# A graph layer in fp32: the add of an edge part between the two products of an older unit on VectorE

## The chip, the cores and the metric

The kernel runs on one core of a Trainium2 chip. Five engines work side by side, each through its own instructions in order: TensorE (PE, matrix products into PSUM), VectorE (DVE), ScalarE (ACT), GpSimd (POOL, here the issuer of gathers) and SyncE (SP, here the issuer of plain DMAs). They wait for each other by semaphores. The metric is the device time of one execution in microseconds, as the median of several runs. The profile is of one execution and has a span, from the first to the last instruction, and a time of its own.

## What is computed

One layer of a graph network over 6250 nodes and 206250 edges with 256 features, all in fp32:

```python
h = relu(layernorm(x))
polarity = clip(edge_attr[:, 0:1], 0.0, 1.0)
e = relu(edge_attr[:, 1:] @ W_e1.T + b_e1) @ W_e2.T + b_e2
edge_emb = (e * (polarity + 0.01)) @ W_le.T + b_le
msg = relu(h[src] + edge_emb)
aggr = segment_sum(msg, dst, num_segments=6250)
out = x + (relu(layernorm((h + aggr) @ W_g1.T + b_g1) * ln_g + ln_b) @ W_g2.T + b_g2)
```

(the layer normalisation's gain and offset stand in the last line for short). The edges are sorted by `dst`. The kernel multiplies `W_e2` and `W_le` together once, so that an edge needs two matrix products: the first layer, 64 to 256, and the edge part, 256 to 256. The edge's factor, `polarity + 0.01`, is applied afterwards, as a product with a scalar for each partition.

## The kernel before

**Tiles.** Edges come in tiles of 128. Two tiles make a unit, 806 in all, two units a block, two blocks a pair. Six blocks make a group, whose messages are summed into one PSUM tile.

**PSUM.** Seven banks (`banks`, `BANKS = 7`) form a ring. Each new use takes the next bank; the matmul that writes it waits for the reader of seven uses ago. An eighth bank, `pd`, holds the sums of two groups.

**A unit's way.**
- `first_layer(q)` (L292): the first layer of a pair, on TensorE. It takes four banks, two for each half `c`. The four results are evicted with bias and Relu, three on ScalarE (L308) and one on VectorE (L305). The first matmul of each half waits for the readers of both its banks.
- `edge_part(u)` (L325): four matmuls into one bank. Then the *add* (L331) on VectorE: bank plus bias, written to `msg[u]` in SBUF, and with it the bank is free.
- `gather` (L634): two indirect DMAs on GpSimd fetch the rows `h[src]` (with `b_le` in them) into `hg[u]`. They are issued in step with TensorE (`in_step`, called at the end of `edge_part`).
- `whole(u)`: two *products* (L685) on VectorE, each `hg = msg * factor + hg` on 128x256, then one Relu (L690) on ScalarE over both.
- `add_up` (L703): selection matrices times `hg`, the sums of a block, on TensorE. `add_pairs` decides how many pairs are summed, from `made`, the number of units whose products are issued.

**The order.** It is written out by hand; the scheduler is off. The main loop goes over u, and each step issues for all engines: `forward(u)` (the edge part of unit u and, in some units, a turn), a *piece*, the products of one or more older units, a part of the node work, and later moves. The products run behind the edge part by `lag` units, which falls from 18 to 1 over the run:

```python
lag = max(LEAST, LEAD - RAW - u // SHRINK) + (by_two(u // 4) and (u + 1) % 8 == TURN)
ready_for = min(u + 1 - lag, 5 * (u + 1 - LEAD) // 4)
while made < ready_for:
    gathers(made + 1)
    whole(made)
    made += 1
```

**Turns.** Between the sixth pair and the sixth from the end (`by_two`), two pairs are turned at once, in units with `u % 8 == 1`: the first layer of one pair (four banks), the sums, the first layer of the next pair (four banks), and two loads of 256 KB on SP's queue (`load_pair`). In the unit before, `u % 8 == 0`, `lag` is one more and no products are issued; in the turn's unit two units' products are. "Unit 0" to "unit 7" below mean `u % 8`.

**Pieces.** `piece()` takes one waiting small step of VectorE: a selection matrix for a block (L663, from `rest`, filled when sums are issued) or a step of the node work that is due (L800, L230). It is called once in a unit, and once more when over six are waiting.

**Node work.** Windows of 128 nodes go through a transpose (L166), a product (L181), normalisation on VectorE and ScalarE (L189 to L193), a transpose (L199), and a last product (L212, L217). `due()` issues one such part in a unit, but none in units 0 and 1. Each takes a bank of the ring.

Of the kernel before, what the change touches and what calls it, by code (L numbers as in the profile page):

```python
# [11 lines left out]
AF = mybir.ActivationFunctionType  # L12
ALU = mybir.AluOpType
# [23 lines left out]
NP = -(-NB // 2)  # L37
# [3 lines left out]
LEAD = 22  # L41
LEAST = 1
# [4 lines left out]
SHRINK = 44  # L47
RAW = 4
# [3 lines left out]
TURN = 1  # L52
# [48 lines left out]
def gnn_kernel(ctx: ExitStack, tc: tile.TileContext, x, src_c, dst_c, dst_r, pol_c, raw_t, w_e1t, w_e2,  # L101
               w_let, w_g1t, w_g2t, vec_c, row_v, x_t, out):
    nc = tc.nc
# [23 lines left out]
    pol_s = const.tile([P, NT], F32, name="pol_s")  # L127
# [106 lines left out]
    NU = 2 * NB  # L234
    fast = ExitStack()
    fast.enter_context(tc.manual_schedule())
    with fast:
# [9 lines left out]
        raw, sel, e1, hg, msg, ms = {}, {}, {}, {}, {}, {}  # L247
# [65 lines left out]
        def plain(u):  # L313

            return u < LEAD and u % 3 == 1

        def edge_part(u):

            nonlocal last_z
            b, v = divmod(u, 2)  # L320
            pz = ps()
            for i in range(2):
                k = (2 * v + i) * P
                for c in range(2):
                    last_z = nc.tensor.matmul(pz[:, i, :], e1[b][:, c, k:k + P], wc_s[:, c, :], start=c == 0, stop=c == 1)  # L325
            ps.wrote(last_z)
            msg[u] = msg_p.tile([P, 2, D], F32, name="msg")
            if plain(u):
                ps.read(nc.scalar.activation(msg[u], pz, AF.Copy))
            else:  # L330
                ps.read(nc.vector.tensor_add(msg[u], pz, bc_s))  # L331
            if v == 1:
                e1.pop(b)
            paced(EDGE, last_z)

        last_z = None
        sums = lambda last: None
        paced = lambda us, behind: None

        def by_two(q):  # L340
            return FEW <= q < NP - FEW
# [65 lines left out]
        with tc.tile_pool(name="p1", bufs=4) as p1, tc.tile_pool(name="p1x", bufs=11) as p1x:  # L407
# [76 lines left out]
            for k in range(len(parts) + 1):  # L484
                last = len(parts) - 1
# [128 lines left out]
        with tc.tile_pool(name="hg", bufs=HG - RAW) as hg_p, tc.tile_pool(name="ms", bufs=4) as ms_p, \  # L614
# [7 lines left out]
            done = {}  # L622
# [18 lines left out]
            def gathers(last):  # L641

                while got < 2 * min(NU, last):
                    gather()
# [29 lines left out]
                elif rest:  # L674
                    rest.popleft()[1]()

            def whole(u):

                m = msg.pop(u)
                if u < RAW:  # L680
                    nc.vector.tensor_add(hg[u], hg[u], ble_b.rearrange("p (o d) -> p o d", o=1).to_broadcast([P, 2, D]))
                if plain(u):
                    nc.vector.tensor_add(m, m, bc_s)
                for i in range(2):
                    product = nc.vector.scalar_tensor_tensor(hg[u][:, i, :], m[:, i, :], pol_s[:, 2 * u + i:2 * u + i + 1],  # L685
                                                   hg[u][:, i, :], op0=ALU.mult, op1=ALU.add)
                    if u == NU - 1:
                        nc.scalar.activation(hg[u][:, i, :], hg[u][:, i, :], AF.Relu)
                if u < NU - 1:
                    done[u] = product, nc.scalar.activation(hg[u], hg[u], AF.Relu)  # L690

            def add_up(b, newest=()):

# [41 lines left out]
            def add_pairs(last=False):  # L735

                nonlocal summed
                whole_groups = []
                pairs = 0
                while summed + pairs < NP and min(4 * (summed + pairs) + 4, NU) < made + last:  # L740
                    pairs += 1
                for _ in range(pairs):
                    newest = done.get(4 * summed + 3, ())
                    for b in (2 * summed, 2 * summed + 1):
                        if b < NB:
                            whole_groups.append(add_up(b, newest))
                            newest = ()
                            if b % L == 0 and group_of(b) + 2 < NG:
                                rest.extend(select(group_of(b) + 2))
                    summed += 1  # L750

                for g in whole_groups:
                    keep(g)
# [158 lines left out]
                    todo.setdefault(now + 1, deque()).extendleft(reversed(fns))  # L912

            gathers(RAW + 1)
            sums = add_pairs
            paced = in_step
            def strips():
                rows_of_edges()
# [13 lines left out]
            for u in range(LEAD, NU):  # L932
                now = u
                forward(u)

                if u >= NU - 24:
                    gathers(4 * summed + HG)

                piece()
                lag = max(LEAST, LEAD - RAW - u // SHRINK) + (by_two(u // 4) and (u + 1) % 8 == TURN)  # L940
                ready_for = min(u + 1 - lag, 5 * (u + 1 - LEAD) // 4)
                while made < ready_for:
                    gathers(made + 1)
                    whole(made)
                    made += 1
                due()
                for fn in moves.pop(now, []):
                    fn()
                if len(rest) > 6:
                    piece()  # L950
                if u == NU - 24:
                    for w in range(NW):
                        if groups_of(w)[-1] == NG - 1:
                            late[w] = node_work(w, True)
                if u == LEAD + 60:
                    flag = nc.values_load(bad_i[0:1, 0:1], min_val=0, max_val=4 * P)
# [209 lines left out]
```

## Time and profile before

| | |
|---|---|
| median of three runs | 2563.11 us (2563.05 to 2566.45) |
| the profiled execution, own time | 2555.42 us |
| its span | 2553.7 us |
| its mean granted TensorE clock | 0.964 |
| ScalarE, Relu of the products (L690) | 805 of 631 ns, 507.6 us |
| VectorE, selection matrices (L663) | 403 of 344 ns, 138.6 us |
| TensorE, edge parts (L325) | 1506.0 us in 6448 instructions |
| TensorE, first layer (L292) | 462.0 us in 1612 instructions |
| TensorE, sums (L703) | 266.0 us in 3216 instructions |

A row of groups names the line, the engine, the operation, what is written and read, the count; after the bar the busy time in us and the mean of one in ns; after the second bar the engine's idle time just before such instructions and what ended it. A row of the timeline has start in us, length, engine, line, operation, count, and in brackets the idle time before it with its releaser. Rows that begin with an engine and a line only are from a view of one line's waiters: total us and times. A row of windows has the stretch, then busy us (and count) of PE, PEld, DVE, ACT and POOL, the granted clock, the DMA share and GB/s. fp32 matmuls stand in the trace as two instructions each. "remote" and "issue" are waits whose end the profile could not place.

### The profile page before, as it was taken

To read this page: it belongs to the slowest core of one execution; us is meant where nothing else is said; L and a number is where in the kernel's file an instruction comes from. 1 tells how busy PE (TensorE), PEld (TensorE's weight loads), DVE (VectorE), ACT (ScalarE), POOL (GpSimd) and SP (SyncE) were. 2 spreads that over 40 slices of the span, in tenths; PEclk is the share of its full clock that TensorE was granted. 3 is DMA by queue.
4 is the path that set the end of the run, shared out by engine and by line. 5 is a ranking of instruction groups with operands and counts; after the bars stand their busy time and mean duration, and the time that the engine had idled before them with its cause. 6 is when DMAs were issued, how large, how long until landed. Compare 5 with 4: busy or idle time off the path is not lost.

```text
span 2553.7 us, 36839 instructions
## 1 busy us (share of the span) xinstructions
PE 2312.4 (91%) x11940; PEld 1603.9 (63%) x11940; DVE 1599.9 (63%) x3705; ACT 1012.7 (40%) x1804; POOL 1630.2 (64%) x1675
## 2 busy tenths in 40 slices
PE   9899889998999989899899989999989999898968
PEld 6666666665656666666666666666656666565646
DVE  7776556665656656565656665666656666666636
ACT  7443334343433434343433433433344334334323
POOL 7666666666666666666666666666666666666661
PEclk9899999999989999999999999999999999999979
DMA  9444444444444444444444444444444444443441
GB/s 306 139 123 127 116 132 131 125 126 134 129 122 137 121 122 130 133 127 116 126 129 123 132 135 118 130 124 136 135 121 124 127 129 142 120 130 114 123 119 42
DMA packets 176431, 330.30 MB, mean 129 GB/s; under 512 B 39056, under 2 KB 98281, under 8 KB 176233
## 3 DMA queue, kind: packets, MB, share of 16 engines
q0 software_dynamic: 77376, 211.39, 29.6%
q1 hardware_dynamic: 97556, 113.22, 13.7%
q10 hardware_dynamic: 1300, 3.28, 0.4%
q8 instruction: 95, 1.56, 0.3%
q14 instruction: 104, 0.84, 0.1%
HBM read 293.92 MB, written 33.82 MB: 128 GB/s over the span
## 4 chain that ended last, share of the span: by engine, by line
PE 77%; DVE 8%; issue 8%; another core or an unknown queue 3%; ACT 2%; DMA 0%; DVEq 0%; ACTq 0%
PE pz L325 48%; PE pz L292 15%; PE pd L703 8%; DVE hg L685 4%; DVE msg L331 2%; PE pz L181 2%; PE pz L212 2%; ACT hg L690 1%; PE pz L166 1%; ACT e L308 1%; DVE sel L663 1%; PE pz L199 0%; DVE xt L230 0%; DVE stb L800 0%
## 5 line engine op out<-in xcount | busy, mean ns | idle before, releaser
L634 POOL DMA_INDIRECT hg<-hb_d,src_s x1604 | 1585.3, 988 | 862.9 <-issue 519.1
L325 PE MATMUL pz<-wc_s,e 128*128 128x256 f32 x6448 | 1506.0, 387 | 60.0 <-issue 46.6
L325 PEld LDWEIGHTS pz<-wc_s,e 128*128 128x128 f32 x6448 | 1225.5, 193 | 344.1 <-issue 130.9
L690 ACT ACTIVATE hg<-hg 128x512 f32<-128x512 f32 x805 | 507.6, 631 | 980.7 <-DVE hg L685 766.0
L331 DVE TENSOR_TENSOR msg<-pz,bc_s 128x512 f32<-128x512 f32 x799 | 545.4, 685 | 379.0 <-PE pz L325 143.0
L685 DVE SCALAR_TENSOR_TENSOR hg<-msg,pol_s,hg 128x256 f32<-128x256 f32 x1612 | 696.5, 479 | 0.8 <-DMA hg<-hb_d,src_s 0.5
L292 PE MATMUL pz<-raw,we_s 64*128 64x512 f32 x1612 | 462.0, 657 | 66.6 <-DVE msg L331 30.1
L308 ACT ACTIVATE e<-pz,vecs 128x512 f32<-128x512 f32 x605 | 372.7, 684 | 256.6 <-remote 110.1
L305 DVE TENSOR_SCALAR e<-pz,vecs 128x512 f32<-128x512 f32 x201 | 150.2, 747 | 503.5 <-remote 176.4
L703 PE MATMUL pd<-hg,sel 128*32 128x256 f32 x3216 | 266.0, 398 | 71.6 <-issue 69.6
L292 PEld LDWEIGHTS pz<-raw,we_s 64*128 64x128 f32 x1612 | 152.3, 196 | 277.5 <-issue 143.5
L703 PEld LDWEIGHTS pd<-hg,sel 128*32 128x32 f32 x3216 | 118.5, 112 | 244.6 <-issue 201.2
L663 DVE SCALAR_TENSOR_TENSOR sel<-iota_w,zero_c,rel 128x128 f32<-128x128 f32 x403 | 138.6, 344 | 0.0
L718 ACT ACTIVATE ms<-pd 128x256 f32<-128x256 f32 x66 | 25.3, 384 | 246.4 <-remote 90.5
L181 PE MATMUL pz<-wg_s,hT 128*128 128x256 f32 (+1 forms) x196 | 54.0, 398 | 17.5 <-issue 7.6
L212 PE MATMUL pz<-wg_s,nT 128*128 128x256 f32 (+1 forms) x196 | 51.5, 385 | 6.4 <-ACT nT L203 4.9
L181 PEld LDWEIGHTS pz<-wg_s,hT 128*128 128x128 f32 (+1 forms) x196 | 35.1, 191 | 33.0 <-ACT hT L170 11.3
L212 PEld LDWEIGHTS pz<-wg_s,nT 128*128 128x128 f32 (+1 forms) x196 | 36.8, 190 | 13.4 <-ACT nT L203 6.4
L444 POOL TENSOR_TENSOR hb<-xt,rows_b 128x256 f32<-128x256 f32 (+1 forms) x49 | 34.1, 728 | 10.8 <-issue 4.4
L800 DVE TENSOR_TENSOR stb<-stb,ab 128x256 f32<-128x256 f32 x94 | 39.2, 417 | 2.6 <-DMA ab<-sum_d 2.6
L203 ACT ACTIVATE nT<-pz,vecs 128x128 f32<-128x128 f32 (+1 forms) x98 | 38.7, 444 | 2.4 <-PE pz L199 2.4
L230 DVE SCALAR_TENSOR_TENSOR xt<-xt,zero_c,rows_b 128x128 f32<-128x128 f32 (+1 forms) x98 | 33.6, 344 | 0.0
(108 smaller groups left out, 378.5 us busy)
## 6 DMA issues: line engine op xcount, KB each, us to landing
raw<-in_raw_t_dram SPq DMA_DIRECT2D x202, 256.0 KB
hg<-hb_d,src_s POOLq DMA_INDIRECT x1604
sum_d<-zrow SPq DMA_DIRECT2D x94, 128.0 KB
ab<-sum_d SPq DMA_DIRECT2D x94, 128.0 KB
sum_d<-ms SPq DMA_DIRECT2D x264, 32.0 KB
hb_d<-hb SPq DMA_DIRECT2D x12, 512.0 KB
xt<-in_x_dram SPq DMA_DIRECT2D x48, 128.0 KB
out_dram<-ot SPq DMA_DIRECT2D x48, 128.0 KB
```

Source lines behind the costliest of these rows:

```text
L181: z = nc.tensor.matmul(ph[:n, 0, :], aT[:, c, :n], wg1_s[:, c, :], start=c == 0 and not bias_by_pe, stop=c == 1)
L212: z = nc.tensor.matmul(po[:n, 0, :], nT[:, c, :n], wg2_s[:, c, :], start=c == 0, stop=c == 1)
L292: z[c] = nc.tensor.matmul(pe[s, c], we1_s[s * F:(s + 1) * F, c * P:(c + 1) * P], raw[q][s * F:(s + 1) * F, :], start=True, stop=True)
L305: a = nc.vector.tensor_scalar(e1[b][:, c, :], pe[s, c], be1_s[:, c:c + 1], 0.0, op0=ALU.add, op1=ALU.max)
L308: a = nc.scalar.activation(e1[b][:, c, :], pe[s, c], AF.Relu, bias=be1_s[:, c:c + 1])
L325: last_z = nc.tensor.matmul(pz[:, i, :], e1[b][:, c, k:k + P], wc_s[:, c, :], start=c == 0, stop=c == 1)
L331: ps.read(nc.vector.tensor_add(msg[u], pz, bc_s))
L634: g = nc.gpsimd.indirect_dma_start(out=hg[u][:, i, :], out_offset=None, in_=hb_d, in_offset=bass.IndirectOffsetOnAxis(ap=src_s[:, 2 * u + ...
L663: nc.vector.scalar_tensor_tensor(sel[g][:, k * S:(k + 1) * S, :], iota_w.rearrange("p (o w) -> p o w", o=1).to_broadcast([P, S, W]), zero_ ...
L685: product = nc.vector.scalar_tensor_tensor(hg[u][:, i, :], m[:, i, :], pol_s[:, 2 * u + i:2 * u + i + 1], hg[u][:, i, :], op0=ALU.mult, op ...
L690: done[u] = product, nc.scalar.activation(hg[u], hg[u], AF.Relu)
L703: z = nc.tensor.matmul(acc[g][j * W:(j + 1) * W, :], sel[g][:, k * S + j, :], m[:, j % 2, :], start=k == 0, stop=b == blocks_of(g)[-1])
```

## The change

In units 2 to 7 of the two-pair part of the run, if one unit's products are due, the first of them is issued before the add of the edge part and the second after it, inside `edge_part`. The piece, that stood between add and products, comes after both. In the turn's unit (`u % 8 == TURN`) and outside the two-pair part the products stay where they were, after `forward(u)` and the piece, but a call of `piece()` now stands between the two products of each unit. `due_at` is the old expression for what is due. `add_pairs` counts as before: inside a unit whose products were issued early, `made` is taken one lower. No operation, tile, DMA or buffer count is changed.

```diff
             msg[u] = msg_p.tile([P, 2, D], F32, name="msg")
+            half_of_products(u, 0)
             if plain(u):
                 ps.read(nc.scalar.activation(msg[u], pz, AF.Copy))
             else:
                 ps.read(nc.vector.tensor_add(msg[u], pz, bc_s))
+            half_of_products(u, 1)
...
-            def whole(u):
-
-                m = msg.pop(u)
+            def products(u, i):
+
+                if i == 0:
+                    opened(u)
+                product = nc.vector.scalar_tensor_tensor(hg[u][:, i, :], msg[u][:, i, :], pol_s[:, 2 * u + i:2 * u + i + 1],
+                                               hg[u][:, i, :], op0=ALU.mult, op1=ALU.add)
+                if u == NU - 1:
+                    nc.scalar.activation(hg[u][:, i, :], hg[u][:, i, :], AF.Relu)
+                elif i == 1:
+                    done[u] = product, nc.scalar.activation(hg[u], hg[u], AF.Relu)
+                if i == 1:
+                    msg.pop(u)
...
+            def whole(u, between=lambda: None):
+
+                products(u, 0)
+                between()
+                products(u, 1)
...
-                while summed + pairs < NP and min(4 * (summed + pairs) + 4, NU) < made + last:
+                while summed + pairs < NP and min(4 * (summed + pairs) + 4, NU) < made - eager + last:
...
+            def due_at(u):
+
+                lag = max(LEAST, LEAD - RAW - u // SHRINK) + (by_two(u // 4) and (u + 1) % 8 == TURN)
+                return min(u + 1 - lag, 5 * (u + 1 - LEAD) // 4)
+
+            def half_now(u, i):
+
+                nonlocal made, eager
+                if i == 0:
+                    eager = by_two(u // 4) and u % 8 != TURN and made < due_at(u)
+                    if eager:
+                        gathers(made + 1)
+                if eager:
+                    products(made, i)
+                    made += i
...
                 piece()
-                lag = max(LEAST, LEAD - RAW - u // SHRINK) + (by_two(u // 4) and (u + 1) % 8 == TURN)
-                ready_for = min(u + 1 - lag, 5 * (u + 1 - LEAD) // 4)
-                while made < ready_for:
+                while made < due_at(u):
                     gathers(made + 1)
-                    whole(made)
+                    whole(made, piece)
                     made += 1
```

`opened(u)` holds what `whole` did first for the earliest units (the bias of `hg` for u < 4, the bias of `msg` where ScalarE had copied it).

12 lines of the change are left out of this document (5 added, 7 removed).

## The prediction

> **What bounds the kernel now.** I read the page first: the engines' busy time, the chain that ended last, the costliest groups.
>
> ```profile
> span 2553.7 us, 36839 instructions
> PE 2312.4 (91%) x11940; PEld 1603.9 (63%) x11940; DVE 1599.9 (63%) x3705; ACT 1012.7 (40%) x1804; POOL 1630.2 (64%) x1675
> PE 77%; DVE 8%; issue 8%; another core or an unknown queue 3%; ACT 2%; DMA 0%; DVEq 0%; ACTq 0%
> L331 DVE TENSOR_TENSOR msg<-pz,bc_s 128x512 f32<-128x512 f32 x799 | 545.4, 685 | 379.0 <-PE pz L325 143.0
> L685 DVE SCALAR_TENSOR_TENSOR hg<-msg,pol_s,hg 128x256 f32<-128x256 f32 x1612 | 696.5, 479 | 0.8 <-DMA hg<-hb_d,src_s 0.5
> L305 DVE TENSOR_SCALAR e<-pz,vecs 128x512 f32<-128x512 f32 x201 | 150.2, 747 | 503.5 <-remote 176.4
> ```
>
> TensorE sets the end: 91% busy and 77% of the chain. Its idle time is 2553.7 - 2312.4 = 241.3 us. VectorE is 63% busy; what matters of it is only when it frees PSUM banks. Its idle time lies in two places: 503.5 us before the second eviction of the first layer (L305), where it has caught up, and 379.0 us before the adds (L331).
>
> Next I asked who waits for an add.
>
> ```profile
>   PEld pz L292: 68.8, 72
>   PE pz L292: 30.1, 26
>   PE pz L325: 0.4, 1
> ```
>
> So TensorE stands still for an add almost nowhere but at the first layer (L292), in a turn of two pairs: 26 times, 30.1 us. Another 72 - 26 = 46 waits of a weight load are covered by matmuls still running. I followed the ring of seven banks back from each of the 26, in order of the banks that TensorE takes. A turn takes eight banks: four for the first pair, then the sums, then four for the second pair. The second half of the first pair needs the add of unit 6 or 7 of the eight-unit period; the first half of the second pair needs that of unit 0. By this 15 of the 26 wait for unit 6 or 7 (21.8 us; the first and last are the upper two rows) and 11 for unit 0 (8.3 us; the lower two).
>
> ```profile
> 173.27 0.70 PE L292 MATMUL pz<-raw,we_s 64*128 64x512 f32 x2 [1.56 <-DVE msg L331]
> ...
> 2350.82 1.22 PE L292 MATMUL pz<-raw,we_s 64*128 64x512 f32 x2 [2.00 <-DVE msg L331]
> ...
> 78.45 0.70 PE L292 MATMUL pz<-raw,we_s 64*128 64x512 f32 x2 [1.32 <-DVE msg L331]
> ...
> 2278.06 0.70 PE L292 MATMUL pz<-raw,we_s 64*128 64x512 f32 x2 [0.24 <-DVE msg L331]
> ```
>
> The timeline of VectorE shows how an add comes to be late.
>
> ```profile
> 1017.95 0.68 DVE L331 TENSOR_TENSOR msg<-pz,bc_s 128x512 f32<-128x512 f32 x1
> 1018.55 0.34 DVE L663 SCALAR_TENSOR_TENSOR sel<-iota_w,zero_c,rel 128x128 f32<-128x128 f32 x1
> 1018.81 0.87 DVE L685 SCALAR_TENSOR_TENSOR hg<-msg,pol_s,hg 128x256 f32<-128x256 f32 x2
> 1019.60 0.34 DVE L663 SCALAR_TENSOR_TENSOR sel<-iota_w,zero_c,rel 128x128 f32<-128x128 f32 x1
> 1019.86 0.68 DVE L331 TENSOR_TENSOR msg<-pz,bc_s 128x512 f32<-128x512 f32 x1
> ...
> 1027.66 0.88 DVE L685 SCALAR_TENSOR_TENSOR hg<-msg,pol_s,hg 128x256 f32<-128x256 f32 x2
> 1031.65 0.69 DVE L331 TENSOR_TENSOR msg<-pz,bc_s 128x512 f32<-128x512 f32 x1 [3.11 <-PE pz L292]
> 1032.26 0.34 DVE L663 SCALAR_TENSOR_TENSOR sel<-iota_w,zero_c,rel 128x128 f32<-128x128 f32 x1
> ```
>
> From start to start an add takes 0.60 us (1017.95 to 1018.55), a piece 0.26, two products 0.79 (1018.81 to 1019.60), so one is 0.40 (rounded up). A unit is 0.60 + 0.26 + 0.79 = 1.65 us of VectorE. TensorE gives one in half of this row, 1.73 us:
>
> ```profile
> 1021.80 3.45 PE pz L325 x16
> ```
>
> VectorE, late after a turn, hardly gains on TensorE between turns. The second of these two is unit 7, over at 1025.25. Yet VectorE stood idle for 3.11 us before its add at 1031.65, and the row names a later matmul as what ended the wait: the signal came late. Such holds decide which adds are late, and nothing in this change touches them.
>
> **The change, step by step.** Instructions added or removed: none. The products (L685), their Relu on ScalarE, the adds and the pieces are all still there, the DMAs are the same, and the forced gathers of a product find their rows already asked for, as they do now. Only VectorE's order moves, and ScalarE's Relu with it.
>
> *Order in units 2 to 7.* Now: add, piece, product, product. Then: product, add, product, piece. Read as a circle, the same work lies between one add and the next, so in the middle of the run nothing changes. The ends of the run change. Ahead of the adds of units 2 to 7 stands one product more (0.40 us), if VectorE is never idle after the turn. Behind the add of unit 7, ahead of that of unit 0, stands one product less.
>
> *What an idle time does.* If VectorE waits at the add of unit k, the leading product now runs inside that wait. The add of k is then no later, nor are those up to 7, and the adds of units 0 and 1 come 0.40 us earlier. I counted the waits by unit: in 82 of 95 turns there is one of at least 0.40 us before an add of units 2 to 7; these are the first and the last.
>
> ```profile
> 90.08 0.69 DVE L331 TENSOR_TENSOR msg<-pz,bc_s 128x512 f32<-128x512 f32 x1 [0.53 <-PE pz L325]
> ...
> 2445.11 0.69 DVE L331 TENSOR_TENSOR msg<-pz,bc_s 128x512 f32<-128x512 f32 x1 [1.85 <-PE pz L212]
> ```
>
> *Term 1, the waits for unit 0.* All 11 of those turns have such an idle time. Eight waits are over 0.40 us and lose 0.40; the other three (0.25, 0.39, 0.24) end: 8 x 0.40 + 0.88 = 4.1 us gained. The bound below is 0, if the earlier signal meets another wait at the same bank.
>
> *Term 2, the waits for units 6 and 7.* In all 15 turns VectorE idled before one of units 2 to 7, in 14 for more than a product, so these waits keep their size; the fifteenth, whose idle time is 0.18, grows by 0.22. Upper bound, were all idle times gone: 15 x 0.40 = 6.0 us lost.
>
> *Term 3, the hidden waits.* The 46 covered weight loads could come out where the add is later. Bounds 0 and 46 x 0.40 = 18.4 us. I take the share of turns without a full idle time, 13 of 95, and as much of each as is exposed now, 26 of 72: 18.4 x 0.14 x 0.36 = 0.9 us lost.
>
> *Moved pieces.* A turn's unit now calls for three pieces, not one, and each brings the adds of units 2 to 5 up to 2 x 0.26 = 0.52 us later, until later units find none left. By unit 6 the count is the same. Where an idle time comes early, the pieces run in it and the adds of 6 and 7 gain up to 0.52 us; I take 0, and keep 15 x 0.52 = 7.8 us gained as a bound.
>
> *Waits that the moved product brings.* The leading product waits for its gathered rows and holds the add behind it, and with it the bank. It moves ahead by an add and a piece, 0.86 us, or by an idle time. Of 1612 products one waits for its rows now, 0.5 us (the L685 row). I take 0. If one in ten of some 570 moved products waited 0.3 us, 17 us of VectorE, and the adds would be late by that.
>
> *The clock.*
>
> ```profile
> core 0: 2553.7 us, clock 0.964
> 1000.00:1002.00 2.00, 0.69 (x2) 0.15 (x1) 0.00 (x0) 0.00 (x0) 0.61 (x1) 1.00 0.43 131
> 1002.00:1004.00 2.00, 1.68 (x4) 1.24 (x5) 1.46 (x5) 0.79 (x2) 0.45 (x1) 0.65 0.00 0
> 1004.00:1006.00 2.00, 2.00 (x6) 0.63 (x5) 2.00 (x6) 0.10 (x1) 1.52 (x2) 0.50 0.23 66
> ```
>
> After a stretch with TensorE idle for two thirds, the granted clock falls to 0.50. Over the run (1 - 0.964) x 2553.7 = 92 us go to this, 92 / 241.3 = 0.38 us for each idle us. On the net of the terms, 4.1 - 0.2 - 0.9 = 3.0 us, that is 1.1 us more; waits of 0.4 us need not reach the threshold, so I take none of it. The Trainium skill ("TensorE: Matmul & The Clock Gate", section "What's actually happening") says that the clock halves after at least one idle window of about 3.4 us. By that rule waits of this size alone halve nothing and the sum stays at 3.0 us; by the proportion it is 4.1. The rows above, which fall to 0.50 after 1.3 us without matmuls in a stretch of 2, ask for less idle time than the rule does, so both stay open.
>
> *Sum.* 3.0 us less. The profiled execution took 2555.4 us by its own time (span 2553.7), 7.7 below the median of the runs, 2563.1; 2555.4 - 3.0 = 2552.4 there, and 2563.1 - 3.0 = 2560.1 for the median. A change under 0.2%, 5.1 us, is what a measurement of this kernel can hardly tell from none; the forecast lies inside it.
>
> **Rivals.**
>
> *Slower: the leading product delays the bank that the turn needs.* Place: the add of unit 6 or 7 ahead of the first pair's second half. Price: term 2 at its bound, 6.0, and of term 3 the share exposed now, 18.4 x 26/72 = 6.6; 12.6 us, and 4.8 of clock at 0.38: 2580. It decides once VectorE has no idle time of 0.40 us left before units 2 to 7. For it: the unit's 1.65 us against 1.73. Against it: 82 of 95.
>
> *Faster: the idle time takes more than one product.* Terms 1 (4.1) and the moved pieces at their bound (7.8), with 4.5 of clock: 16.4 us, 2547. For it: 379.0 us of idle time before the adds, most of it after the turn's work is queued. Against: the pieces before a late hold are already done by then.
>
> *No effect.* TensorE waits at the same bank for ScalarE or a held signal: 2563.
>
> *The gathers.* The leading product waits for its rows: 17 us on VectorE; with the exposed share 26/72 it is 6 us, 2569.
>
> **How the numbers follow.** Forecast with no effect beside it: 0.34 (their own range 2558 to 2568). Faster 0.36, over everything between 5 us and 16 us. Slower 0.30: 0.25 for the delayed bank, 0.05 for the gathers. The likeliest single case, the sum, gives 2560. The faster and slower mechanisms have 0.66 between them because each needs only some of its bound to pass 5 us; the changed order shifts every turn against the holds, and the three runs alone spread by 3.4 us. Range: the faster price, 2547, and the slower one short of its full clock share, 2577.
>
> **What would show it.** On VectorE the two products of units 2 to 7 stand apart with an add between. Right if the waits of L292 for L331 fall from 26 towards 18, with those for unit 0 mostly gone, and idle time before L331 falls as idle time before L685 appears nowhere. The slower rival shows as more and longer waits of the first pair's second half; the gather rival as idle time of L685 before a DMA; the faster one as less than 25 us of waits and a mean clock over 0.964. The forecast is wrong in its basis if the idle time of TensorE moves by over 10 us at lines other than L292.

## The result, and the profile after

| | before | after | ratio after / before, 95% interval |
|---|---|---|---|
| first chip, median of 12 runs each | 2561.98 us | 2561.93 us | 0.9998 (0.9974 to 1.0023) |
| profiled execution, own time | 2555.42 us | 2561.1 us | |
| its span, its mean granted clock | 2553.7 us, 0.964 | 2559.2 us, 0.960 | |

No difference that can be told. The forecast was 2560.0 us; it asked for 3.0 us less, and the interval runs from 6.7 us less to 5.9 us more. The single profiled execution is 5.7 us longer than that of before, which is inside the spread of the runs (2547.52 to 2571.9 us for the changed kernel).

From the page of the changed kernel: span, busy times, the chain by engine, and the groups of the adds (now L332), the products (now L684) and the second eviction of the first layer (L305).

```profile
span 2559.2 us, 36843 instructions
PE 2342.4 (92%) x11940; PEld 1616.9 (63%) x11940; DVE 1599.0 (62%) x3705; ACT 1018.6 (40%) x1804; POOL 1645.3 (64%) x1675
PE 80%; DVE 8%; issue 8%; another core or an unknown queue 2%; ACT 2%; DMA 1%; POOL 0%; DVEq 0%; ACTq 0%; POOLq 0%
L332 DVE TENSOR_TENSOR msg<-pz,bc_s 128x512 f32<-128x512 f32 x799 | 545.7, 687 | 357.5 <-remote 117.6
L684 DVE SCALAR_TENSOR_TENSOR hg<-msg,pol_s,hg 128x256 f32<-128x256 f32 x1612 | 736.2, 479 | 4.2 <-issue 2.2
L305 DVE TENSOR_SCALAR e<-pz,vecs 128x512 f32<-128x512 f32 x201 | 150.3, 748 | 530.5 <-PE pz L292 168.5
```

The counts are the same. The products' busy time rose from 696.5 to 736.2 us although one still takes 479 ns and all of VectorE is busy no longer than before (1599.0 against 1599.9): two products that follow each other overlap by 0.08 us, and products that stand apart overlap with the add and the piece instead. The idle time before the adds fell by 21.5 us (379.0 to 357.5), and the idle time before L305 rose by 27.0 (503.5 to 530.5). By unit, over units 24 to 779 of both traces, the idle time before the adds of units 2 to 7 fell from 267.9 to 216.2 us, and that before the adds of unit 0 rose from 47.8 to 81.7: the leading products run in the first, and what is saved behind the add of unit 7 shows before the add of unit 0 and ahead of the turn.

Who waits for the adds, by the view of the add's line:

```profile
  PEld pz L292: 53.1, 59
  PE pz L292: 22.9, 16
  PE pz L325: 0.3, 1
```

And who waits for the products, by the view of theirs:

```profile
  PEld pz L292: 19.9, 35
  PE pz L292: 6.9, 4
```

Before, the first layer waited 26 times, 30.1 us, for adds, and by the same view of the products 2 times, 2.6 us, for those. Now it is 16 + 4 = 20 times and 22.9 + 6.9 = 29.8 us, against 28 and 32.7. (A wait is put down to the instruction that ended closest to its end. A product that now follows the add at once takes some of the add's waits on itself, so the two views have to be added up.)

The timeline of VectorE in the changed kernel shows the new order, product, add, product, piece, and what a held signal still does:

```profile
1029.03 0.68 DVE L332 TENSOR_TENSOR msg<-pz,bc_s 128x512 f32<-128x512 f32 x1
1029.63 0.48 DVE L684 SCALAR_TENSOR_TENSOR hg<-msg,pol_s,hg 128x256 f32<-128x256 f32 x1
1030.02 0.35 DVE L666 SCALAR_TENSOR_TENSOR sel<-iota_w,zero_c,rel 128x128 f32<-128x128 f32 x1
1030.28 0.48 DVE L684 SCALAR_TENSOR_TENSOR hg<-msg,pol_s,hg 128x256 f32<-128x256 f32 x1
1033.44 0.69 DVE L332 TENSOR_TENSOR msg<-pz,bc_s 128x512 f32<-128x512 f32 x1 [2.67 <-PE pz L292]
```

TensorE over the same time, in its own timeline (the row at 1023.47 is units 6 and 7, that at 1027.78 units 0 and 1):

```profile
1023.47 3.62 PE L325 MATMUL pz<-wc_s,e 128*128 128x256 f32 x16
...
1027.78 3.62 PE L325 MATMUL pz<-wc_s,e 128*128 128x256 f32 x16
1031.33 1.13 PE L292 MATMUL pz<-raw,we_s 64*128 64x512 f32 x4
1034.18 1.13 PE L292 MATMUL pz<-raw,we_s 64*128 64x512 f32 x4 [1.72 <-DVE msg L332]
```

The add at 1033.44 is that of unit 7. Its matmuls end with the row at 1023.47, at 1027.09, and the leading product is done at 1030.28 + 0.48 = 1030.76. Even so the add starts only at 1033.44, after 2.67 us of idle time and 6.35 us after its matmuls, and TensorE stands still for 1.72 us at the second half of the first pair. The 0.40 us product in front of the add costs nothing here, and its being there saves nothing either: the late signal decides.

The largest waits of TensorE in the kernel before, outside what the prediction looked at (total us, times, longest):

```profile
PE pd L703 <- issue: 69.6, 106, 1.7
PE pz L325 <- issue: 46.6, 88, 1.7
...
PE pz L292 <- issue: 19.6, 27, 2.2
```

and in the changed kernel:

```profile
PE pd L718 <- issue: 74.4, 122, 1.8
PE pz L292 <- issue: 27.3, 45, 2.7
PE pz L325 <- issue: 25.0, 57, 1.0
```

TensorE's idle time went from 241.3 to 2559.2 - 2342.4 = 216.8 us, and most of that is the 21.6 us at the edge parts, with no releaser that the profile could place. The idle time differs by as much between profiles of one kernel: the kernel before has 241.3, 212.2 and 216.3 us on the first chip and in the second and third group below.

TensorE's busy time went up by 30.0 us, and that recurs: by 21.8 us in the second group and 26.3 in the third. Part of it lies at the sums, here before and after:

```profile
L703 PE MATMUL pd<-hg,sel 128*32 128x256 f32 x3216 | 266.0, 398 | 71.6 <-issue 69.6
```

```profile
L718 PE MATMUL pd<-hg,sel 128*32 128x256 f32 x3216 | 279.2, 401 | 77.7 <-issue 74.4
```

The sums and the idle time before them take 337.6 us before and 356.9 after; in the second group 336.6 and 375.0, in the third 369.6 and 386.0. With the products apart alone (below) they take 378.4 and 389.2, with the piece alone 327.4. So the longer sums go with the products apart in all five profiles. But the kernel before scatters by 33 us from chip to chip, and why the sums should take longer was not tried.

### The profile page after: what moved, and what is told of

It reads as the page before. It is cut to its first block, busy times and chain, and to the rows that moved or that the text cites. A ratio compares the mean times of both kernels' runs of the same rounds, so it can differ in the third digit from the quotient of the medians.

```text
span 2559.2 us, 36843 instructions
## 1 busy us (share of the span) xinstructions
PE 2342.4 (92%) x11940; PEld 1616.9 (63%) x11940; DVE 1599.0 (62%) x3705; ACT 1018.6 (40%) x1804; POOL 1645.3 (64%) x1675
## 4 chain that ended last, share of the span: by engine, by line
PE 80%; DVE 8%; issue 8%; another core or an unknown queue 2%; ACT 2%; DMA 1%; POOL 0%; DVEq 0%; ACTq 0%; POOLq 0%
PE pz L325 49%; PE pz L292 16%; PE pd L718 9%; DVE hg L684 3%; DVE msg L332 2%; PE pz L181 2%; PE pz L212 2%; PE pz L166 1%; ACT e L308 1%; DVE st L151 1%; ACT hg L689 0%; PE pz L199 0%; DVE sel L666 0%; DMA hg<-hb_d,src_s 0%
## 5 line engine op out<-in xcount | busy, mean ns | idle before, releaser
L332 DVE TENSOR_TENSOR msg<-pz,bc_s 128x512 f32<-128x512 f32 x799 | 545.7, 687 | 357.5 <-remote 117.6
L684 DVE SCALAR_TENSOR_TENSOR hg<-msg,pol_s,hg 128x256 f32<-128x256 f32 x1612 | 736.2, 479 | 4.2 <-issue 2.2
L292 PE MATMUL pz<-raw,we_s 64*128 64x512 f32 x1612 | 478.8, 651 | 62.8 <-issue 27.3
L308 ACT ACTIVATE e<-pz,vecs 128x512 f32<-128x512 f32 x605 | 372.7, 684 | 331.5 <-remote 156.0
L305 DVE TENSOR_SCALAR e<-pz,vecs 128x512 f32<-128x512 f32 x201 | 150.3, 748 | 530.5 <-PE pz L292 168.5
L718 PE MATMUL pd<-hg,sel 128*32 128x256 f32 x3216 | 279.2, 401 | 77.7 <-issue 74.4
L292 PEld LDWEIGHTS pz<-raw,we_s 64*128 64x128 f32 x1612 | 156.5, 193 | 289.8 <-issue 187.3
L181 PEld LDWEIGHTS pz<-wg_s,hT 128*128 128x128 f32 (+1 forms) x196 | 35.7, 191 | 25.8 <-ACT hT L170 11.2
```

The costliest lines, as they stand in the source:

```text
L181: z = nc.tensor.matmul(ph[:n, 0, :], aT[:, c, :n], wg1_s[:, c, :], start=c == 0 and not bias_by_pe, stop=c == 1)
L292: z[c] = nc.tensor.matmul(pe[s, c], we1_s[s * F:(s + 1) * F, c * P:(c + 1) * P], raw[q][s * F:(s + 1) * F, :], start=True, stop=True)
L305: a = nc.vector.tensor_scalar(e1[b][:, c, :], pe[s, c], be1_s[:, c:c + 1], 0.0, op0=ALU.add, op1=ALU.max)
L308: a = nc.scalar.activation(e1[b][:, c, :], pe[s, c], AF.Relu, bias=be1_s[:, c:c + 1])
L684: product = nc.vector.scalar_tensor_tensor(hg[u][:, i, :], msg[u][:, i, :], pol_s[:, 2 * u + i:2 * u + i + 1], hg[u][:, i, :], op0=ALU.mul ...
L718: z = nc.tensor.matmul(acc[g][j * W:(j + 1) * W, :], sel[g][:, k * S + j, :], m[:, j % 2, :], start=k == 0, stop=b == blocks_of(g)[-1])
```

## The experiments

Kernels of one group ran on the same chip and share the runs of the kernel before. "TensorE held" below means what the prediction called a held signal: VectorE waits although the matmuls have ended. From the traces I counted, besides the views, the *bank waits*: first-layer matmuls that start within 0.15 us of the end of the last reader of their banks, after over 0.10 us of idle TensorE, by the unit of that reader. By this count the kernel before has 20 for units 6 and 7 (27.2 us) and 16 for unit 0 (9.0 us), a few more than the prediction's 15 and 11 because it does not ask what releaser the view names.

### First group: what a product ahead of the add costs

On this chip the kernel before took 2137.89 us (median of 15 runs, 2135.07 to 2144.36), 424 us less than on the first one. The four expectations were written from the traces of the first chip.

**Both products ahead of the add** in units 2 to 7 (an edit of the changed kernel):

```diff
             msg[u] = msg_p.tile([P, 2, D], F32, name="msg")
             half_of_products(u, 0)
+            half_of_products(u, 1)
             if plain(u):
...
                 ps.read(nc.vector.tensor_add(msg[u], pz, bc_s))
-            half_of_products(u, 1)
```

> The changed kernel, but in units 2 to 7 both products stand ahead of the add: twice the dose of the order. My theory: the adds of units 0 and 1 come up to 0.8 us earlier than before the change and those of units 2 to 5 up to 0.8 us later; the first layer's waits for unit 0 stay at about 5 or fall (16 before, 5 after the change), those for units 6 and 7 stay at about 20 and 25 to 35 us, because late signals set them; time within 10 us of both kernels. The rival of the delayed bank: each product ahead of the add of unit 6 or 7 costs 0.4 us more in every one of those waits, 8 us and more, with the clock 15 us: 2575 or more.

Measured: 2158.02 us, ratio 1.0088 (1.0074 to 1.0103), 20 us slower.

**Two small operations more ahead of the add** (an edit of the kernel before; 128x128 each, no one reads them, 0.52 us by the pitch of a piece):

```diff
+            def one_more(u):
+
+                if u >= 32 and by_two(u // 4) and u % 8 not in QUIET:
+                    for _ in range(2):
+                        nc.vector.scalar_tensor_tensor(extra, zrow[:, :P], zero_c, zrow[:, P:], op0=ALU.add, op1=ALU.add)
...
             msg[u] = msg_p.tile([P, 2, D], F32, name="msg")
+            ahead_of_add(u)
```

> The kernel before with two more operations on VectorE (128x128, 0.26 us each from start to start) ahead of the add in units 2 to 7 from unit 32 on: 0.52 us a unit, 3.1 us a turn, some 295 us in all. It asks what lateness of VectorE costs at all. My theory: the idle times before the adds of units 2 to 7 (2.8 us a turn before) take up about half, the adds of units 0 and 1 come some 1.5 us later, and the first layer waits for them in most turns: 60 to 150 us slower, with idle time before L331 down from 379 to under 200 us. If VectorE's order and lateness did not matter because TensorE waits for other things: under 15 us. If VectorE were the bound: 250 us or more.

Measured: 2175.14 us, ratio 1.0163 (1.0146 to 1.0180), 37 us slower, between the two cases of the expectation (60 or more, under 15).

**One product less** in units 2 to 7 (an edit of the kernel before):

```diff
                 for i in range(2):
+                    if i == 0 and by_two(now // 4) and now % 8 not in QUIET:
+                        continue
```

> The kernel before with the first product of each unit left out in units 2 to 7 (that half of the messages stays the gathered rows): VectorE has 0.40 us less in a unit, 2.4 us a turn, some 225 us in all. My theory: the adds are on time unless a signal is late; the waits of the first layer for an add of unit 0 go, those for units 6 and 7 keep half their size or more (late signals); 15 to 40 us faster. If lateness of VectorE in itself set the waits: all of the 30 us and their clock go, and the covered waits too, 60 us or more faster. If it does not matter at all: within 8 us.

Measured: 2129.26 us, ratio 0.9952 (0.9937 to 0.9967), 9 us faster, less than the 15 to 40 expected.

**No loads of edge features** from the ninth pair on (an edit of the kernel before):

```diff
+                if q < 8:
+                    kept[q % 4] = raw[q] = ld.tile([P, 512], F32, name="raw")
+                    nc.sync.dma_start(out=raw[q], in_=raw_t[q])
+                else:
+                    raw[q] = kept[q % 4]
```

> The kernel before with the loads of the edge features left out from the ninth pair on (later pairs use the features of the first eight): 51 MB less, and no 512 KB burst in a turn. It asks where the late signals come from. If the burst holds them back: VectorE's idle time before the first layer's second eviction (L305, 503 us) falls under 250 us, the waits between TensorE's matmuls in the turn named issue (L703 69.6 us) fall under half, and the time by 80 us or more. If they come from elsewhere (the gathers, the engines' own instructions): L305 keeps over 400 us and the time moves under 25 us.

Measured: 2137.37 us, ratio 1.0000 (0.9991 to 1.0009). It could not answer its question, since there is nothing left here to remove: TensorE is not held on this chip. But as its time is that of the kernel before and its order of instructions too, its profile stands for that kernel here, as far as a kernel with 51 MB less to load can. From its page (adds are L336, products L690), and from its view of VectorE's waits:

```profile
PE 2114.9 (99%) x11940; PEld 1551.5 (73%) x11940; DVE 1620.8 (76%) x3705; ACT 1013.6 (47%) x1804; POOL 1608.8 (75%) x1675
L336 DVE TENSOR_TENSOR msg<-pz,bc_s 128x512 f32<-128x512 f32 x799 | 542.9, 682 | 9.6 <-PE pz L330 9.0
```

```profile
DVE hg L690 <- DMA hg<-hb_d,src_s: 227.0, 347, 2.3
...
DVE msg L336 <- PE pz L330: 9.0, 20, 1.2
```

The row of the adds in the same view of the kernel before, on the first chip:

```profile
DVE msg L331 <- PE pz L325: 143.0, 82, 5.3
```

TensorE is busy 99% of the span of 2134.8 us. The idle time before the adds is 9.6 us, not 379.0, so the reserve on which terms 1 and 2 of the prediction rest is gone. In its place VectorE waits 347 times, 227.0 us, for *gathered rows*, ahead of a product; in the profile of before on the first chip that was one wait of 0.5 us. In the order of before these waits lie behind the add of their unit, and the first layer waits for an add only 6 times, 5.3 us in all.

The page, the wait view of VectorE and its timeline of the kernel with both products ahead show what happens when they come to lie in front (adds L333, products L684):

```profile
PE 2120.6 (98%) x11940; PEld 1550.5 (72%) x11940; DVE 1616.3 (75%) x3705; ACT 1019.8 (47%) x1804; POOL 1627.1 (76%) x1675
```

```profile
DVE hg L684 <- DMA hg<-hb_d,src_s: 233.0, 308, 3.0
```

```profile
1014.27 0.48 DVE L684 SCALAR_TENSOR_TENSOR hg<-msg,pol_s,hg 128x256 f32<-128x256 f32 x1
1016.78 0.48 DVE L684 SCALAR_TENSOR_TENSOR hg<-msg,pol_s,hg 128x256 f32<-128x256 f32 x1 [2.04 <-DMA hg<-hb_d,src_s]
1017.19 0.68 DVE L333 TENSOR_TENSOR msg<-pz,bc_s 128x512 f32<-128x512 f32 x1
```

VectorE stands 2.04 us in front of a product whose rows are not there, with the add behind it. In the mean over the run the adds of units 4 to 7 start 1.3 to 2.0 us later after their matmuls than in the kernel without loads (unit 4: 0.63 to 2.62 us; unit 7: 2.70 to 4.03). Two products account for 0.80 of it; the rest, 0.5 to 1.2, fits the waits for rows, but was not separated from them. The first layer pays, by the wait views of TensorE, first both products ahead, then two operations more:

```profile
PE pz L292 <- DVE msg L333: 20.7, 17, 2.8
```

```profile
PE pz L292 <- DVE msg L332: 28.2, 40, 2.8
PE pz L292 <- ACT e L308: 8.1, 8, 1.9
```

What follows. Where TensorE is not held, work in front of an add does cost time: the idle time that was to take it is not there. For both products ahead a second step comes in that this expectation had not listed, though the prediction has it as a rival: the wait for gathered rows. How the 20 us divide between the two products and the rows was not measured. Two operations of 0.52 us without rows to wait for brought 37 us, far less than I had thought, since VectorE is not full: its waits for rows fell to 20.1 us and so paid for most of it. And with one product fewer the first layer waited once, 1.3 us, for an add, instead of 6 times: in this state its waits for adds follow VectorE's load. TensorE, at 99%, had only 19.9 us of idle time to give.

### Second group: the parts of the change, apart

The chip of this group held TensorE again: 2522.63 us for the kernel before (35 runs, 2510.57 to 2546.53). The expectations were written for the state of the group above. Three of the four theories miss: the kernel before was to take 2138 us, and the changed kernel and the one with the products apart were to be slower by 3 us or more. Only that for the piece alone, within 2 us, holds. (The ratios below are not quotients of the medians beside them.)

**The kernel before** and **the changed kernel** as they are:

> The kernel before, unchanged, for a profile beside the next three. In the runs of both_ahead, extra_op, one_less and no_raw_loads TensorE was 98 to 99% busy and the signals were not late. My theory: here too VectorE has no idle time of 0.40 us before an add of units 2 to 7 in more than 5 of 95 turns, and the first layer's waits for an add come to under 8 us; 2138 us. If those waits came from the order and not from late signals: 25 us or more.

> The changed kernel, unchanged. My theory, with the case that the slower rival of the prediction names (no idle time left that takes the leading product): the adds of units 2 to 7 come 0.40 us later and up to 0.9 in units 2 and 3, those of units 0 and 1 not earlier; the first pair's second half waits 5 to 12 us more than before: 0.2 to 0.5% slower, about half of what both_ahead cost (18.8 us, measured). If the order costs nothing here either: within 0.1%. The prediction's sum, 3 us faster, needs idle times that I do not expect here.

Measured: before 2520.02 us, 0.9994 (0.9972 to 1.0016); changed 2520.94 us, 0.9979 (0.9957 to 1.0001). The 0.2% that may lie between them is not resolved.

**The products apart, without the piece between** (an edit of the changed kernel):

```diff
                 while made < due_at(u):
                     gathers(made + 1)
-                    whole(made, piece)
+                    whole(made)
```

> The changed kernel without the piece between the products of a turn's unit: the products of units 2 to 7 stand apart, nothing else moves. My theory: the leading product costs at the first layer, so this is as slow as after_again or a little less (3 to 10 us over before). If the moved pieces are what costs: within 2 us of before.

Measured: 2523.73 us, 1.0006 (0.9989 to 1.0023).

**The piece between the products alone** (an edit of the kernel before; products stay behind the add):

```diff
-            def whole(u):
+            def whole(u, between=lambda: None):
...
+                    if i == 0:
+                        between()
...
-                    whole(made)
+                    whole(made, piece if now % 8 == TURN or not by_two(now // 4) else lambda: None)
```

> The kernel before with a piece between the two products of each unit in a turn's unit and outside the two-pair part, and the adds where they were. My theory: pieces done by unit 4 instead of unit 6 change no add of units 6, 7, 0 and 1: within 2 us of before. If they are what costs in after_again: as slow as that.

Measured: 2523.01 us, 0.9987 (0.9961 to 1.0013).

The bank waits by unit tell the parts apart where the times do not. Unit 0: 16 before (7.4 us), 5 changed (3.3), 4 with the products apart (5.2), 12 with the piece alone (9.3). So it is with the products apart that the waits for unit 0 end. Units 6 and 7: 9 before (8.0 us), 16 changed (15.6), 18 with the products apart (24.1), 13 with the piece alone (14.2). Both kinds together are 25, 21, 22 and 25: in part the turn may only be held up earlier, for units 6 and 7 instead of unit 0.

### Third group: a third chip, and a version meant to be better

This chip held TensorE as well: before 2523.34 us (35 runs, 2513.81 to 2533.92).

> The kernel before, for its profile on the same chip as the three others. Ratio 1.000 within 0.1%. Its first-layer waits for adds are 15 or more in unit 0 of the two-pair turn, against 6 or fewer in the changed kernel's profile.

> The changed kernel once more, to see whether its time stands apart from the kernel before where VectorE has little idle time. The first chip's profile had 241.3 us of PE idle and 357.5 us of VectorE idle before the add, and the two kernels could not be told apart (2561.93 against 2561.98 us). Where TensorE is held up little (below 60 us of idle, a time near 2138 us), my theory has no idle time left that takes the leading product: each add of units 6 and 7 comes up to 0.40 us later, and the changed kernel is 0.2 to 0.5% slower (4 to 11 us). The rival that idle VectorE time takes the product anyway expects 0.1% or less on either side. Where TensorE is held up much (150 us of idle and over), both expect a difference inside 0.2%, with the waits of unit 0 at about a third of the kernel before and those of units 6 and 7 no fewer.

> The changed kernel with both products of the older unit behind one another after the add, or rather with the leading product still ahead of the add and no small piece between the products in the turn's unit: the other part of the change taken back. If the piece costs or brings nothing (its 0.26 us lies behind the add, ahead of a product that nobody waits for), this stands within 0.1% of the changed kernel. If the piece keeps the Relu of the older unit late and through it the sum of pairs, it is faster than the changed kernel by 0.2% or more.

The edit of the third is that of the products apart, above. Measured: before 2525.23 us, 1.0006 (0.9983 to 1.0029); changed 2518.93 us, 0.9974 (0.9961 to 0.9987); apart 2523.29 us, 0.9998 (0.9980 to 1.0016). The first layer's waits for adds, in the same order, by the wait views of the three:

```profile
PE pz L292 <- DVE msg L331: 26.8, 23, 2.9
```

```profile
PE pz L292 <- DVE msg L332: 11.2, 9, 2.6
```

```profile
PE pz L292 <- DVE msg L332: 30.5, 22, 4.5
```

The views of the products add 8.9, 0.8 and 0.9 us, so that the sums are 35.7, 12.0 and 31.4. Bank waits: unit 0 14, 4 and 7 times (10.3, 4.5 and 5.0 us); units 6 and 7 18, 6 and 22 times (24.1, 6.8 and 26.9 us). The kernel before has 14 waits for unit 0, one short of what was expected. The changed kernel is a little faster than the 0.2% expected, and its waits for units 6 and 7 fell, where they were to be no fewer. The kernel with the products apart was to be level with the changed kernel or faster, and is 4 to 6 us slower.

The second and third chip together give 24 runs of the changed kernel with a mean of 2519.8 us, 24 with the products apart at 2524.0, and 92 of before at 2524.1: the changed kernel is 4.3 us faster (plus or minus 2.6, twice the standard error), the one with the products apart 0.1 (2.8), and the piece makes 4.2 (3.2) of difference. By chip the changed kernel is faster than before by 2.4 (4.3) and 6.2 (2.9) us, and on the first chip by 0.4 (5.7); the piece makes 2.4 (4.5) and 6.0 (4.6). So the gain rests mainly on the third chip, and the two chips were put together only after their results were known.

**Products ahead of the turn** (an edit of the kernel before): in the unit of a two-pair turn the products that are due come ahead of the turn's evictions, where VectorE is idle, and their Relus stay behind it.

```diff
             edge_part(u)
             if u % 4 == TURN:
+                ahead_of_turn(u)
                 turn_of(u // 4)
...
+            def products_first(u):
+
+                if by_two(u // 4) and u % 8 == TURN:
+                    for m in range(made, due_at(u)):
+                        gathers(m + 1)
+                        whole(m)
...
                 while made < due_at(u):
                     gathers(made + 1)
-                    whole(made)
+                    if made not in ready_products:
+                        whole(made)
+                    rest_of(made)
                     made += 1
```

(`whole` now only issues the products, and `rest_of` the Relu.)

> The kernel before, with the products of the older units that fall due in the unit of a two-pair turn issued ahead of the turn's first-layer evictions, where VectorE stands idle for TensorE anyway (365 to 530 us before those evictions over the run), and their Relus left where they were. The adds themselves keep their place ahead of all products. My theory: VectorE has four products (1.60 us) less to do behind the turn, so the adds of units 6, 7 and 0 come up to 1.6 us earlier and most of the first-layer waits for adds go: 8 to 20 us faster (0.3 to 0.9%) where TensorE is held up little, not under 0.1% where it is held up much. Rival: the evictions of the turn come later by the products, so TensorE waits there instead, and the time is the same or up to 10 us more.

Measured: 2532.62 us, 1.0029 (1.0009 to 1.0049): slower, by 7 to 9 us. From its page, and the mean clock of its core:

```profile
PE 2334.0 (92%) x11940; PEld 1617.1 (64%) x11940; DVE 1610.1 (63%) x3705; ACT 994.0 (39%) x1804; POOL 1637.1 (64%) x1675
L331 DVE TENSOR_TENSOR msg<-pz,bc_s 128x512 f32<-128x512 f32 x799 | 546.8, 687 | 500.9 <-PE pz L325 223.5
L305 DVE TENSOR_SCALAR e<-pz,vecs 128x512 f32<-128x512 f32 x201 | 150.1, 748 | 361.8 <-PE pz L292 136.1
```

```profile
core 0: 2538.3 us, clock 0.958
```

It does what it says: the idle time before L305 is 361.8 us (458.9 in the profile of before on this chip) and has moved to the adds (500.9 against 396.3). The adds of units 2, 3 and 4 start earlier, 1.41, 1.55 and 1.90 us after their matmuls (2.30, 2.42 and 2.28 before), but that of unit 7 only 3.95 (4.21): by then most of the lead is gone, presumably to held signals. The first layer's waits for adds fell from 26.8 to 15.5 us (with those for products, from 35.7 to 20.8), TensorE's idle time from 2520.6 - 2304.3 = 216.3 to 2538.3 - 2334.0 = 204.3, and yet TensorE is busy 29.7 us longer, at a clock of 0.958 instead of 0.967. The rival had the time nearly right, but its mechanism, TensorE waiting for the turn's evictions, does not show either (3.8 us for L308, against 6.6). Why less waiting goes with a lower clock here was not tried and is open. No version that beats the changed kernel came out of this.

## Why the prediction was right, and where it was not

*What bounds the kernel.* Right: TensorE's idle time, with only the first layer waiting for adds. It held on three of four chips. The idle time at lines other than L292 did move by over 10 us (edge parts, 46.6 to 25.0), which the prediction named as a sign against its basis. The profiles of before speak against reading it so: the same wait was 46.3 us in the second group and 13.3 in the third. It scatters by more than the whole change.

*Order in units 2 to 7, and the idle times that take the product.* The mean time from the end of a unit's matmuls to the start of its add went from 4.88 to 4.60 us for unit 0, from 4.24 to 3.88 for unit 1 and from 2.80 to 3.12 for unit 2, on the first chip; units 3 to 5 are 0.1 to 0.2 later and unit 7 0.38 earlier. The earlier adds of units 0 and 1 are the shape that was predicted; the earlier add of unit 7 is not. The sign named for it, idle time before the adds falling while none appears before the products, is in the page (379.0 to 357.5; 0.8 to 4.2).

*Term 1, unit 0, 4.1 us gained.* Right in mechanism and about right in size: 9.0 to 6.1 us on the first chip, 7.4 to 3.3 and 10.3 to 4.5 on the other two, 4.3 in the mean. The waits fell from 16, 16 and 14 to 5, 5 and 4, and with the products apart alone to 4 and 7. Of all steps this one repeated best. In the mean the adds of unit 0 do not start earlier with the products apart alone (4.47 to 4.61 and 4.50 to 4.77 us after their matmuls), presumably since late signals set most of them. What moved are the close cases. In the profiles of before, in one turn of ten, the add of unit 0 ends 0.20 to 0.24 us or more after TensorE is free for the bank; in those of the changed kernel the same tenth begins at 0.26 to 0.60 us ahead of it (0.33 and 0.07 with the products apart alone).

*Term 2, units 6 and 7, 0.2 us lost.* Not settled by the changed kernel: 27.2 to 26.4, 8.0 to 15.6 and 24.1 to 6.8 us, changes of both signs, larger than the term and its bound of 6.0. Two profiles of before alone differ by 19. With the products apart alone the waits are at 24.1 and 26.9 us against 8.0 and 24.1, so a loss there can be set against the gain at unit 0, and the times agree: 0.1 us of difference.

*Term 3 and the clock.* Weight loads that wait while matmuls still run: 46 for adds and 25 - 2 = 23 for products before, 59 - 16 = 43 and 35 - 4 = 31 now, 69 against 74. None of them can be seen to have come out; 0.9 us lost was within what cannot be told. The mean clock fell a little, 0.964 to 0.960, while the idle time fell by 24.5 us, so the proportion of clock to idle time does not hold from one execution to the next. To have taken nothing for it was right, the 0.38 was not a price. The rows by which the prediction left the matter open average over 2 us. In the profile of before the clock is halved 36 times, mostly for 3.41 or 6.83 us, and in the 3.41 us ahead TensorE was idle for 0.81 to 2.75 us in 35 cases and all the time in one. So far less than 3.4 us of idle time was enough here, and how much is needed does not come out of these rows.

*Moved pieces, taken at 0.* This is the step that failed, inside its bound of 7.8 us. "By unit 6 the count is the same" is wrong: in the instruction order of units 24 to 779 the kernel before has 289 selection matrices from behind the add of unit 1 to that of unit 6, the changed one 379, and from there to the next unit 1 it has 109, the changed one 21 (the steps of node work in that stretch, 90, are the same in both). So the adds of units 7, 0 and 1 have nearly no selection matrix right in front of them any more. Counted from the turn on, though, more of them stand ahead of the adds of units 7 and 0 than before (398 against 354 and 375), so these adds gain only if VectorE idles on the way, the condition that the prediction gives for its bound. The runs of the second and third chip put 4.2 us (plus or minus 3.2) on the piece, by the kernels with and without it; the piece alone, on the order of before, gave 1.9 (4.0), which neither confirms nor excludes it. That the piece is what makes the changed kernel faster there is therefore likely, not shown.

*What has no term.* The prediction puts nothing on the sums. With the products apart they took 16 to 42 us more, idle time included, than in the kernel before on the same chip, in every pair of profiles, and the whole was no slower. What pays for it, and whether it is more than scatter, is open.

*Waits of the moved product, taken at 0.* Right where TensorE is held: 2 waits, 1.6 us, for rows. But the reason given, one wait in 1612, belongs to that state alone. On the chip without holds it is 347 waits, and the kernel with both products ahead paid 20 us, by the mechanism of the rival on gathers, that of the delayed bank, or both. The changed kernel itself was never met there, so whether it is slower on such a chip was not measured.

*The sum.* 3.0 us less was asked for; on the first chip 0 was measured, with an interval that holds it, on the other two 4.3 (2.6). That the time fell into the range says little for the terms: single runs of either kernel on that chip reach from 2547.52 to 2575.0 us, nearly the whole range. The chance of no difference was the smaller of the two large ones, and the reasons given for the spread, holds that shift with every execution, are what the groups showed.

## What to carry to other kernels

Before costing a reorder by the idle time of one profile, ask what makes that idle time and whether it will be there in the next run: here it came from late signals that one chip does not have, and without them a wait that had been invisible, 347 times for gathered rows, lay in its place. Work that can wait for a DMA is safer behind the instruction that frees a bank than ahead of it: two products ahead cost 20 us on the chip without holds, though how much of it is the rows was not separated. And when terms of 0.2 to 6 us are at stake in a kernel whose executions scatter by 20 us, count the waits that the change should end (16 to 5 on two chips, 14 to 4 on the third), and those that it may bring elsewhere, before reading the total.

## What was not expected of the hardware

The same kernel took 2562, 2523, 2523 and 2138 us on four chips, steadily on each. On the last one TensorE was busy 99% at a granted clock of 0.998, and the longest wait of an add for its edge part was 1.2 us; on the first chip the clock was 0.964 and that wait up to 5.3 us (no profile has the kernel before itself on the last chip; the one without loads stands for it). Between the two profiles lie 241.3 - 19.9 = 221 us of idle TensorE, and 2312.4 - 2114.9 = 198 us by which the same 11940 instructions were busy longer; the lower mean clock, 0.034 of some 2300 us, accounts for about 80 of these. Much of the rest is spacing: the sums' matmuls last nearly the same (398 and 382 ns in the mean), but cover 266.0 us on the first chip and 194.5 on the last, since they start further apart and overlap less. What holds the signals, and whether the lower clock is their cause or their effect, was not found; nor can it be told whether the signal or the matmul itself is late, since the profile models the ends of matmuls. Leaving out the loads of edge features ran on the chip that has no holds, and no other cause was tried.
